# Self attention inside a pipelined perceiver layer: its scores on other PSUM banks and directly behind a step's logits, its softmax in two calls, its normalisations split from the products ahead of them

## The chip, the cores and the metric

One core of a Trainium2 chip runs the whole program. The metric is the time of one execution on the device, in microseconds. Three runs of the kernel before took 690.27 to 690.64 us, with a median of 690.4 us. Times inside an execution come from one profiled execution.

## The reference

The program computes one layer of a perceiver: a cross attention, a self attention and a quantised feed-forward net, each with a residual. The input x has 32 batches of 64 latents with 128 features; the context has 32 batches of 1601 tokens, of which a mask leaves out a part. All is float32.

```python
def cross(ctx, latents, mask):                   # 16 heads of 64
    xn, ln = layernorm(ctx, gx, bx), layernorm(latents, gl, bl)
    q, kv  = ln @ Wq, concatenate((xn, ln), axis=1) @ Wkv
    sim    = where(mask_full, -big, (q * scale) @ k.T)
    return layernorm((softmax(sim) @ v) @ Wout, go, bo)

def self_attention(x):                           # 16 heads of 8
    q, k, v = x @ Wq.T + bq, x @ Wk.T + bk, x @ Wv.T + bv
    scores  = q @ k.T / sqrt(8) + slopes * (pos_k - pos_q)
    return softmax(scores) @ v @ Wo.T + bo

x = x + cross(ctx, _layernorm(x), mask)
x = x + self_attention(_layernorm(x))
x = x + ffn(_layernorm(x))                       # fake-quantised, silu gate, 352 hidden
```

## The kernel before, in words

**Tiling.** Batches are sorted by how many context positions they need, and long ones are paired with short ones: 16 pairs of two batches, so that the 2 x 64 latents of a pair fill the 128 partitions. A batch is handled with a capped number of keys (its 64 latents among them): 448 for the first nine, 320 for eight, 192 for seven and 64 for the last eight. Pair t holds ranks t and 31 - t, so the early pairs have 448 and 64 keys, and the late ones 320 and 192. A switch chooses one of three variants of the whole attention by the lengths that the mask shows; this input takes the capped variant, called narrow in the code.

**PSUM.** All eight banks are given out by three rings: `bank_s` turns through two banks, `bank_t` and `bank_m` through three each. A call takes the next bank of its ring, and whoever writes into it first waits until the last reader of that bank's previous tile is done.

**Steps.** Pair t has eight steps, one for each two heads of the cross attention. The loop at L900 goes over all 128 steps and some more for the drain. In each it first calls `logits`, then the functions that a table `later` lists for that step, in the order in which they were listed. The framework turns this into one fixed instruction order for each engine, and sets the semaphores.

**The cross attention of a step.** `logits` multiplies the step's queries with the keys of each of the two batches (L568, PE, into a `bank_s` bank). VectorE adds the mask's addend and finds the row's least value while it evacuates the bank (L571, tile `s`, statistic `low`), ScalarE takes the exponential and sums it (L576, `den`), and VectorE inverts the sums and normalises (L582 `rden`, L585). Two steps later `turned` transposes the probabilities on PE (L604 for short batches, L614 for long ones, into `bank_t`), and ScalarE copies them out (L607, L615, tile `pT`). Another step or two later `attend` multiplies them with the normalised context (L632, into `bank_m`), and VectorE copies the product out (L637, `oT`).

**The next pair's preparation**, beside the steps of this pair: `latents` normalises its latents (`norm1`, L477, tile `ln`), `latents_T` transposes them (L243 from `ln`, into `bank_t`), `prepare` normalises its context tokens: VectorE takes the moments, L465 and GpSimd's power L469 give `rstd`, VectorE L498 gives `shift`, ScalarE applies both (L502), VectorE applies gain and bias (L224, L225), and GpSimd fills in the latents (L507) and turns the mask into addends (L510 to L520). `keys_T` transposes the tokens, `queries` multiplies the latents with the folded query weights (L544, four calls, into `bank_m`; ScalarE copies to `qT`, L548).

**The self attention of a finished pair** runs beside the steps of the next pair. Its pieces are put into the table by `chain`, a tuple of offsets from the step e in which the next pair begins: `project` in two calls (L663; behind the last come the moments of the product, gain and residual, L671 to L677, and a second normalisation to the tile `xl`, L680, with GpSimd's L469 in each), `self_T` (L689, transpose of `xl`), `self_qkv` (L700 to L728), `self_softmax` (L731), `self_pT` twice (transposes of the probabilities), `self_values` (L788, sums by L795) and `self_out` (L804, then a normalisation into `x3` and its largest absolute value for the quantisation, L806 to L809). `self_softmax` issues 8 small matmuls for scores into four banks (L738), one from `bank_s`, one from `bank_t` and two from `bank_m`; then, for each half of the 16 heads, two bias additions on VectorE (L750, tile `p`, each over four heads), a maximum (L754), a subtraction (L755) and an exponential on ScalarE (L759). For all pairs but the last two `chain` is

```python
elif t < NP - 2:
    chain = (4, 5, 7, 8, 10, 13, 14, 15, 16)
else:
    chain = (None, None, 4, 5, 6, 8, 8, 9, 10)
```

so that scores and softmax fall into step e + 10, the third step of the pair after the next. For the last two pairs the projection is spread over the pair's own steps in four parts. Behind the last step the feed-forward net follows, which needs the maximum over all pairs.

Of the kernel before, what the change touches and what calls it, by code (L numbers as in the profile page):

```python
# [8 lines left out]
FP = mybir.dt.float32  # L9
U8 = mybir.dt.uint8  # L10
I32 = mybir.dt.int32
AF = mybir.ActivationFunctionType
# [14 lines left out]
H = 16  # L27
# [10 lines left out]
def perceiver_layer(  # L38
# [21 lines left out]
    def bank_t():  # L60
        return ps_t.tile([P, 512], FP, tag="t", name="bank_t")

    def bank_m():
        return ps_m.tile([P, 512], FP, tag="m", name="bank_m")

    def bank_s():
        return ps_s.tile([P, 512], FP, tag="s", name="bank_s")
# [318 lines left out]
    def attention(actx, name, caps):  # L386
# [263 lines left out]
        def norm1(dst, src, twice=False):  # L650

            mean, rstd = moments(src, twice)
            nc.vector.tensor_scalar(dst, src, mean, rstd, ALU.subtract, ALU.mult)
# [4 lines left out]
        def project(t, part, parts=2):  # L658
            if part == 0:
                own[t] = bank_m()  # L660
            pm, oT = own[t], oTs[t]
            for h in range(H // parts * part, H // parts * (part + 1)):
                nc.tensor.matmul(  # L663
                    pm[:, :D], lhsT=oT[:, h].rearrange("p u i -> p (u i)"), rhs=b_sb[:, h, :],
                    start=(h == 0), stop=(h == H - 1),
                )
            if part < parts - 1:
                return
            oTs.pop(t)

            o = two.tile([P, D], FP, tag="o", name=f"o{t}")  # L671
            mean, rstd = moments(pm[:, :D])
            nc.vector.scalar_tensor_tensor(
                o, pm[:, :D], mean, go_r, ALU.subtract, ALU.mult
            )
            nc.vector.scalar_tensor_tensor(
                x1[:, t, :], o, rstd, x1[:, t, :], ALU.mult, ALU.add  # L677
            )
            xl = two.tile([P, D], FP, tag="xl", name=f"xl{t}")
            norm1(xl, x1[:, t, :])  # L680

            nc.gpsimd.tensor_tensor(x1[:, t, :], x1[:, t, :], sbo_r, ALU.add)
            own[t] = xl
# [44 lines left out]
                )  # L728
            own[t] = q, kx

        def self_softmax(t):  # L731
            q, kx = own[t]

            ps = [bank_s(), bank_t(), bank_m(), bank_m()]
            for u in range(2):
                for r in range(4):
                    rows = slice(32 * r, 32 * r + 32)
                    nc.tensor.matmul(  # L738
                        ps[r][u * SL : (u + 1) * SL, : 4 * SL],
                        lhsT=q[rows, u * SL : (u + 1) * SL],  # L740
                        rhs=kx[rows, :, u, :],
                        start=True, stop=True,
                    )
            p = two.tile([P, H, SL], FP, tag="p", name=f"p{t}", bufs=1)
            stat = small.tile([P, H], FP, tag="stat", name="stat")
            for g in range(2):
                hs = slice(g * 8, g * 8 + 8)
                for r in (2 * g, 2 * g + 1):
                    hr = slice(4 * r, 4 * r + 4)
                    nc.vector.tensor_tensor(  # L750
                        p[:, hr], ps[r][:, : 4 * SL].rearrange("p (h k) -> p h k", k=SL),
                        bias[:, hr], ALU.add,
                    )
                nc.vector.tensor_reduce(stat[:, hs], p[:, hs], AX.X, ALU.max)  # L754
                nc.vector.tensor_tensor(  # L755
                    p[:, hs], p[:, hs],
                    stat[:, hs].unsqueeze(2).to_broadcast([P, 8, SL]), ALU.subtract,
                )
                nc.scalar.activation(p[:, hs], p[:, hs], AF.Exp)  # L759
            own[t] = p  # L760

        def self_pT(t, g):

# [38 lines left out]
        def self_out(t):  # L802
            po = bank_m()
            nc.tensor.matmul(po[:, :D], lhsT=own.pop(t), rhs=swT[:, 3, :], start=True, stop=True)  # L804
            nc.vector.tensor_tensor(x1[:, t, :], po[:, :D], x1[:, t, :], ALU.add)
            norm1(x3[:, t, :], x1[:, t, :])  # L806
            nc.vector.tensor_reduce(
                tops[:, t : t + 1], x3[:, t, :], AX.X, ALU.max, apply_absolute_value=True
            )  # L809
# [20 lines left out]
        for t in range(NP):  # L830
            s0, e = CH * t, CH * (t + 1)
            if not narrow:
                chain = (4, 5, 9, 10, 12, 16, 17, 18, 19)
            elif t < NP - 2:
                chain = (4, 5, 7, 8, 10, 13, 14, 15, 16)
            else:
                chain = (None, None, 4, 5, 6, 8, 8, 9, 10)
            if chain[0] is None:
                for i in range(4):
                    at(s0 + 5 + 2 * i, project, t, i, 4)  # L840
            else:
                at(e + chain[0], project, t, 0)
                at(e + chain[1], project, t, 1)
            if t == NP - 1:
                for k in range(3):
                    at(e + chain[2], ffn_turn, k)
            for k, (f, *more) in zip(
                chain[2:],
                (
                    (self_T,), (self_qkv,), (self_softmax,), (self_pT, 0), (self_pT, 1),  # L850
                    (self_values,), (self_out,),
                ),
            ):
                at(e + k, f, t, *more)
            if t + 1 < NP:
                wait = 0 if narrow else 6
                at(s0 + wait, latents, t + 1)
                at(s0 + wait + 2, latents_T, t + 1)
                for i in range(4):
                    at(e - 6 + i if not narrow else e - 5 + i, queries, t + 1, 4 * i)  # L860

            if narrow:
                for u in range(2):
                    if t + 1 < NP:
                        at(s0 + 1 + 2 * u, prepare, t + 1, u)
                        at(s0 + 5 + u, keys_T, t + 1, u)
                    if t + 2 < NP:
                        at(s0 + 5, load, t + 2, u)
            else:
                for u in range(2):  # L870
                    if t + 1 < NP:
                        at(s0 + 2, lambda t, u: load_x(t, u, batch(t, u)), t + 1, u)
                    if (t, u) != (NP - 1, 1):
                        nxt = (t + u, 1 - u)
                        at(s0 + 8 * u + 3, load, *nxt)
                        at(s0 + 8 * u + 5, prepare, *nxt)
                        at(s0 + 8 * u + 6, keys_T, *nxt)
# [22 lines left out]
        for i in range(max(later) + 1):  # L900
            if i < len(steps):
                logits(*steps[i])
            for f, args in later.get(i, ()):
                f(*args)

    early.close()
# [158 lines left out]
```

## Time and profile before

| | |
|---|---|
| median of three runs | 690.4 us (690.27 to 690.64) |
| the profiled execution | 692.31 us |
| its span, first to last instruction | 690.3 us |
| mean granted TensorE clock | 0.961 |
| recorded instructions | 14206 |
| data moved by DMA | 11.98 MB |

The profiled execution lasted 2.0 us more than its span, which is start and end around the instructions; times inside it are counted from the span's first instruction. The page cuts the span into 40 slices of 17.3 us. A digit is the busy share of an engine in a slice in tenths, and PEclk is the clock that TensorE was granted, in tenths of full speed:

```profile
PE   4598999999998989898999999999999999954975
...
DVE  4487777787868797878778888888888778644673
ACT  2386667666675766675766767676766566512441
POOL 1338320211111112121111212020202000010002
PEclk9599999999999999999999999999999999975988
DMA  4520100000001010100000010000000000000002
```

The first two slices load and prepare, the slices from about the third to the 35th are the pairs, and the last ones are the drain of the last pair and the feed-forward net. PE, DVE, ACT and POOL are TensorE, VectorE, ScalarE and GpSimd. In the lines of a timeline the columns are: start in us, duration in us, engine, line, operation, output <- inputs, tile sizes, how many times in a row, and in brackets how long the engine was idle before it and what ended that. A row of the waits has an engine's tile and line that waited, what it waited for, and then the total in us, the number of times and the longest.

### The profile page before, as it was taken

The numbers are of one execution on the slowest core, as the hardware profiler recorded it, in microseconds if no ns is written. First come the engines' busy times: TensorE is split into PE (matmuls) and PEld (weight loads), VectorE is DVE, ScalarE is ACT, GpSimd is POOL, SyncE is SP. The second block draws the span as 40 slices with busy tenths as digits, with TensorE's granted clock in tenths as the row PEclk, the third lists the DMA queues.
The fourth block names the chain that finished last, engine by engine and source line by source line (L and its number), as shares of the span: only waits on it lengthen the run. The fifth ranks groups of instructions, "written<-read, shape, count | busy, mean of one in ns | idle before, by whom it ended". The sixth has DMA issues, their size and how long they took to land.

```text
span 690.3 us, 14206 instructions
## 1 busy us (share of the span) xinstructions
PE 620.7 (90%) x4798; PEld 496.9 (72%) x4798; DVE 518.7 (75%) x1992; ACT 409.8 (59%) x1096; POOL 130.0 (19%) x273
## 2 busy tenths in 40 slices
PE   4598999999998989898999999999999999954975
PEld 3576878777786868686878888888887886843335
DVE  4487777787868797878778888888888778644673
ACT  2386667666675766675766767676766566512441
POOL 1338320211111112121111212020202000010002
PEclk9599999999999999999999999999999999975988
DMA  4520100000001010100000010000000000000002
GB/s 103 118 56 0 25 1 24 2 24 1 24 2 23 2 30 1 24 1 20 5 11 14 11 15 8 18 7 19 5 24 1 1 1 1 1 1 3 1 0 62
DMA packets 20580, 11.98 MB, mean 17 GB/s; under 512 B 7748, under 2 KB 20036, under 8 KB 20500
## 3 DMA queue, kind: packets, MB, share of 16 engines
q1 hardware_dynamic: 19476, 10.02, 6.4%
q10 hardware_dynamic: 864, 0.82, 0.4%
q8 instruction: 40, 0.66, 0.4%
q14 instruction: 40, 0.33, 0.2%
q0 software_dynamic: 160, 0.16, 0.1%
HBM read 9.94 MB, written 1.05 MB: 16 GB/s over the span
## 4 chain that ended last, share of the span: by engine, by line
PE 49%; DVE 26%; ACT 8%; POOL 5%; issue 5%; DMA 2%; SPq 0%; POOLq 0%; DVEq 0%; ACTq 0%
PE bank_m L632 11%; PE bank_s L568 10%; PE bank_m L663 6%; PE bank_m L544 5%; ACT s L576 5%; DVE s L571 5%; POOL rstd L469 5%; DVE s L585 5%; PE bank_t L614 4%; PE bank_s L971 3%; PE bank_t L243 3%; DVE oT L637 2%; PE bank_m L998 2%; PE bank_t L604 2%; PE bank_m L788 1%
## 5 line engine op out<-in xcount | busy, mean ns | idle before, releaser
L576 ACT ACTIVATE s<-s,low 128x512 f32<-128x512 f32 (+3 forms) x256 | 143.8, 563 | 100.7 <-DVE low L571 87.5
L568 PE MATMUL bank_s<-xT,qT 128*128 128x512 f32 (+3 forms) x512 | 170.6, 449 | 20.6 <-DVE p L750 11.3
L632 PE MATMUL bank_m<-pT,xn 128*128 128x256 f32 x656 | 166.6, 381 | 1.6 <-ACT pT L615 1.4
L568 PEld LDWEIGHTS bank_s<-xT,qT 128*128 128x128 f32 x512 | 88.5, 194 | 77.8 <-DVE p L750 21.5
L469 POOL TENSOR_TENSOR rstd<-rstd,mhalf 128x1 f32<-128x1 f32 (+2 forms) x96 | 61.1, 638 | 411.7 <-DVE rstd L465 387.3
L632 PEld LDWEIGHTS bank_m<-pT,xn 128*128 128x128 f32 x656 | 118.2, 190 | 18.8 <-ACT pT L615 3.4
L571 DVE CUSTOM_DVE_ANT_0 s<-bank_s,ad 128x512 f32<-128x512 f32 (+3 forms) x256 | 121.0, 486 | 8.7 <-PE bank_s L568 7.9
L615 ACT COPY pT<-bank_t 128x512 f32<-128x512 f32 (+1 forms) x136 | 70.4, 523 | 51.5 <-PE bank_t L614 51.3
L585 DVE TENSOR_SCALAR s<-s,rden 128x512 f32<-128x512 f32 (+3 forms) x256 | 89.6, 391 | 2.0
L614 PE MATMUL bank_t<-ident,s 128*128 128x128 f32 x480 | 75.3, 273 | 0.0
L544 PE MATMUL bank_m<-lnT,a_sb 128*128 128x128 f32 x512 | 70.8, 284 | 0.4 <-ACT lnT L244 0.4
L614 PEld LDWEIGHTS bank_t<-ident,s 128*128 128x128 f32 x480 | 60.6, 141 | 13.6 <-issue 1.0
L544 PEld LDWEIGHTS bank_m<-lnT,a_sb 128*128 128x128 f32 x512 | 65.4, 201 | 0.7 <-ACT lnT L244 0.7
L663 PE MATMUL bank_m<-b_sb,oT 128*128 128x128 f32 x512 | 63.3, 276 | 0.5 <-DVE oT L637 0.5
L663 PEld LDWEIGHTS bank_m<-b_sb,oT 128*128 128x128 f32 x512 | 60.0, 192 | 1.7 <-DVE oT L637 1.3
L637 DVE COPY oT<-bank_m 128x256 f32<-128x256 f32 x128 | 53.2, 415 | 10.5 <-PE bank_m L632 10.2
L502 ACT ACTIVATE xn<-xn,shift,rstd 128x128 f32<-128x128 f32 x82 | 36.6, 490 | 25.5 <-DVE shift L498 25.4
L576 ACT ACTIVATION_READ_ACCUMULATOR s<-s,low 128x1 f32 x256 | 48.4, 189 | 0.0
L548 ACT COPY qT<-bank_m 128x512 f32<-128x512 f32 x64 | 37.4, 584 | 16.2 <-PE bank_m L544 15.8
L582 DVE RECIPROCAL rden<-den 128x2 f32<-128x2 f32 x128 | 20.4, 159 | 30.2 <-ACT s L576 29.4
L604 PE MATMUL bank_t<-ident,s 128*128 128x128 f32 x176 | 29.0, 273 | 0.0
L607 ACT COPY pT<-bank_t 128x256 f32<-128x256 f32 (+1 forms) x60 | 28.0, 466 | 0.0
(179 smaller groups left out, 853.5 us busy)
## 6 DMA issues: line engine op xcount, KB each, us to landing
xn<-in_ctx_dram SPq DMA_DIRECT2D x9, 192.0 KB, 2.4
x<-in_x_dram SPq DMA_DIRECT2D x32, 32.0 KB, 2.3
xn<-in_ctx_dram SPq DMA_DIRECT2D x32, 32.0 KB, 2.0
xn<-in_ctx_dram SPq DMA_DIRECT2D x8, 128.0 KB, 2.0
out_dram<-y SPq DMA_DIRECT2D x18, 32.0 KB, 1.9
wk_sb<-in_L_xattn_Wkv_dram ACTq DMA_DIRECT2D x1, 512.0 KB, 4.2
wq_sb<-in_L_xattn_Wq_dram SPq DMA_DIRECT2D x1, 512.0 KB, 5.1
wv_sb<-in_L_xattn_Wkv_dram SPq DMA_DIRECT2D x1, 512.0 KB, 5.3
```

The costliest lines, as they stand in the source:

```text
L469: nc.gpsimd.tensor_tensor(rstd, rstd, mhalf[:, :n], ALU.pow)
L544: nc.tensor.matmul(pm[:, j * P : (j + 1) * P], lhsT=a_sb[:, h4 + j, :], rhs=lnTs[t], start=True, stop=True,)
L568: nc.tensor.matmul(ps[:, : e - k], lhsT=w, rhs=xTs[t, u][:, k:e], start=True, stop=True)
L571: nc.vector.tensor_tensor_reduce(out=s[:, k:e], in0=ps[:, : e - k], in1=addends[u][t % NA][:, k:e], scale=-1.0, scalar=3e38 if j == 0 else ...
L576: nc.scalar.activation(s, s, AF.Exp, bias=low[:, len(pieces) - 1 :], scale=-1.0, accum_out=den[:, i : i + 1],)
L585: nc.vector.tensor_scalar_mul(s, s, rden[:, i : i + 1])
L604: nc.tensor.transpose(bt[:, n, o, :], s[:, n * P : (n + 1) * P], ident)
L614: nc.tensor.transpose(bt[:, j - n, :], s[:, j * P : (j + 1) * P], ident)
L615: nc.scalar.copy(pT[:, n:e, odd, :], bt[:, : e - n, :])
L632: nc.tensor.matmul(po[:, : 2 * P], lhsT=xn[:k, n, :], rhs=pT[:k, n].rearrange("p o c -> p (o c)"), start=(n == 0), stop=(n == len(tiles) - 1),
L637: nc.vector.tensor_copy(oTs[t][:, 2 * c : 2 * c + 4, u, :], po[:, : 2 * P].rearrange("p (h i) -> p h i", i=SL),)
L663: nc.tensor.matmul(pm[:, :D], lhsT=oT[:, h].rearrange("p u i -> p (u i)"), rhs=b_sb[:, h, :], start=(h == 0), stop=(h == H - 1),)
```

## The change

Four things are done. `project` no longer issues the normalisations behind its product; a new function `project_norm` does, listed directly behind the second call and in the same step. Likewise `ffn_norm` takes the normalisation and maximum out of `self_out`, in the same step. `self_softmax` is split: `self_scores` issues the score matmuls and all four bias additions, and takes two `bank_t` and two `bank_m` banks and none of `bank_s`; `self_softmax(t, g)` issues maximum, subtraction and exponential of one half, with a statistics tile of its own, in step e + 11 where the pieces stood in e + 10 (for the last two pairs in e + 6, as the scores). And the loop over steps puts `self_scores` ahead of all other functions of its step, so it comes directly behind the logits. The offsets of all the other pieces are as before. The other variants' offsets change alike; they don't run on this input.

```diff
--- before.py
+++ after.py
@@ -664,9 +664,11 @@
                     pm[:, :D], lhsT=oT[:, h].rearrange("p u i -> p (u i)"), rhs=b_sb[:, h, :],
                     start=(h == 0), stop=(h == H - 1),
                 )
-            if part < parts - 1:
-                return
-            oTs.pop(t)
+            if part == parts - 1:
+                oTs.pop(t)
+
+        def project_norm(t):
+            pm = own[t]
 
             o = two.tile([P, D], FP, tag="o", name=f"o{t}")
             mean, rstd = moments(pm[:, :D])
@@ -728,10 +730,10 @@
                 )
             own[t] = q, kx
 
-        def self_softmax(t):
+        def self_scores(t):
             q, kx = own[t]
 
-            ps = [bank_s(), bank_t(), bank_m(), bank_m()]
+            ps = [bank_t(), bank_t(), bank_m(), bank_m()]
             for u in range(2):
                 for r in range(4):
                     rows = slice(32 * r, 32 * r + 32)
@@ -742,22 +744,24 @@
                         start=True, stop=True,
                     )
             p = two.tile([P, H, SL], FP, tag="p", name=f"p{t}", bufs=1)
-            stat = small.tile([P, H], FP, tag="stat", name="stat")
-            for g in range(2):
-                hs = slice(g * 8, g * 8 + 8)
-                for r in (2 * g, 2 * g + 1):
-                    hr = slice(4 * r, 4 * r + 4)
-                    nc.vector.tensor_tensor(
-                        p[:, hr], ps[r][:, : 4 * SL].rearrange("p (h k) -> p h k", k=SL),
-                        bias[:, hr], ALU.add,
-                    )
-                nc.vector.tensor_reduce(stat[:, hs], p[:, hs], AX.X, ALU.max)
+            for r in range(4):
+                hr = slice(4 * r, 4 * r + 4)
                 nc.vector.tensor_tensor(
-                    p[:, hs], p[:, hs],
-                    stat[:, hs].unsqueeze(2).to_broadcast([P, 8, SL]), ALU.subtract,
-                )
-                nc.scalar.activation(p[:, hs], p[:, hs], AF.Exp)
+                    p[:, hr], ps[r][:, : 4 * SL].rearrange("p (h k) -> p h k", k=SL),
+                    bias[:, hr], ALU.add,
+                )
             own[t] = p
+
+        def self_softmax(t, g):
+
+            p = own[t]
+            stat = small.tile([P, H // 2], FP, tag="stat", name="stat")
+            hs = slice(g * 8, g * 8 + 8)
+            nc.vector.tensor_reduce(stat, p[:, hs], AX.X, ALU.max)
+            nc.vector.tensor_tensor(
+                p[:, hs], p[:, hs], stat.unsqueeze(2).to_broadcast([P, 8, SL]), ALU.subtract
+            )
+            nc.scalar.activation(p[:, hs], p[:, hs], AF.Exp)
 
         def self_pT(t, g):
 
@@ -803,6 +807,8 @@
             po = bank_m()
             nc.tensor.matmul(po[:, :D], lhsT=own.pop(t), rhs=swT[:, 3, :], start=True, stop=True)
             nc.vector.tensor_tensor(x1[:, t, :], po[:, :D], x1[:, t, :], ALU.add)
+
+        def ffn_norm(t):
             norm1(x3[:, t, :], x1[:, t, :])
             nc.vector.tensor_reduce(
                 tops[:, t : t + 1], x3[:, t, :], AX.X, ALU.max, apply_absolute_value=True
@@ -830,11 +836,11 @@
         for t in range(NP):
             s0, e = CH * t, CH * (t + 1)
             if not narrow:
-                chain = (4, 5, 9, 10, 12, 16, 17, 18, 19)
+                chain = (4, 5, 5, 9, 10, 12, 12, 12, 16, 17, 18, 19, 19)
             elif t < NP - 2:
-                chain = (4, 5, 7, 8, 10, 13, 14, 15, 16)
+                chain = (4, 5, 5, 7, 8, 10, 11, 11, 13, 14, 15, 16, 16)
             else:
-                chain = (None, None, 4, 5, 6, 8, 8, 9, 10)
+                chain = (None, None, 3, 4, 5, 6, 6, 6, 8, 8, 9, 10, 10)
             if chain[0] is None:
                 for i in range(4):
                     at(s0 + 5 + 2 * i, project, t, i, 4)
@@ -843,12 +849,13 @@
                 at(e + chain[1], project, t, 1)
             if t == NP - 1:
                 for k in range(3):
-                    at(e + chain[2], ffn_turn, k)
+                    at(e + chain[3], ffn_turn, k)
             for k, (f, *more) in zip(
                 chain[2:],
                 (
-                    (self_T,), (self_qkv,), (self_softmax,), (self_pT, 0), (self_pT, 1),
-                    (self_values,), (self_out,),
+                    (project_norm,), (self_T,), (self_qkv,), (self_scores,), (self_softmax, 0),
+                    (self_softmax, 1), (self_pT, 0), (self_pT, 1), (self_values,), (self_out,),
+                    (ffn_norm,),
                 ),
             ):
                 at(e + k, f, t, *more)
@@ -900,7 +907,8 @@
         for i in range(max(later) + 1):
             if i < len(steps):
                 logits(*steps[i])
-            for f, args in later.get(i, ()):
+
+            for f, args in sorted(later.get(i, ()), key=lambda x: x[0] is not self_scores):
                 f(*args)
 
     early.close()
```

Line numbers behind L666 differ by up to 8 in the changed kernel: the scores' matmuls are L740 there, the bias additions L749, maximum L760, subtraction L761, exponential L764.

## The prediction

> **What bounds the kernel now.** I read the page's busy rows and chain first, then who waits for whom on PE, then the timelines of two pairs: an early one (448 and 64 keys, 135.5 to 171.6) and a late one (320 and 192 keys, 430 to 500).
>
> ```profile
> PE 620.7 (90%) x4798; PEld 496.9 (72%) x4798; DVE 518.7 (75%) x1992; ACT 409.8 (59%) x1096; POOL 130.0 (19%) x273
> ...
> PE 49%; DVE 26%; ACT 8%; POOL 5%; issue 5%; DMA 2%; SPq 0%; POOLq 0%; DVEq 0%; ACTq 0%
> ```
>
> PE is busiest, yet half of the chain that ended last lies elsewhere. PE's two largest repeated waits are these (total, times, longest):
>
> ```profile
> PE bank_s L568 <- DVE p L750: 11.3, 12, 1.3
> PE bank_s L568 <- DVE low L571: 9.0, 10, 1.8
> ```
>
> The first is what the change is aimed at: logits need a ps_s bank that the self attention's scores hold until VectorE has added the bias. The second shows something else: logits that wait for VectorE's previous evacuation. Both stand in each early pair:
>
> ```profile
> 136.82 1.35 PE L568 MATMUL bank_s<-xT,qT 128*128 128x512 f32 x4 [0.86 <-DVE low L571]
> ...
> 142.79 0.49 PE L568 MATMUL bank_s<-xT,qT 128*128 128x128 f32 x2 [1.05 <-DVE p L750]
> ```
>
> Now VectorE in that pair:
>
> ```profile
> 142.35 0.39 DVE L750 TENSOR_TENSOR p<-bank_s,bias 128x256 f32<-128x256 f32 x1
> ...
> 152.35 0.16 DVE L498 SCALAR_TENSOR_TENSOR shift<-mv,rstd 128x4 f32<-128x4 f32 x1 [1.20 <-POOL rstd L469]
> ...
> 154.94 0.17 DVE L582 RECIPROCAL rden<-den 128x2 f32<-128x2 f32 x1 [1.27 <-ACT s L576]
> ...
> 156.55 0.69 DVE L224 TENSOR_TENSOR xn<-xn,gx_r 128x512 f32<-128x512 f32 x1 [0.73 <-ACT xn L502]
> ...
> 159.25 0.68 DVE L571 CUSTOM_DVE_ANT_0 s<-bank_s,ad 128x512 f32<-128x512 f32 x1
> ...
> 161.29 0.35 DVE L653 TENSOR_SCALAR xl<-x,mv,rstd 128x128 f32<-128x128 f32 x1 [0.67 <-POOL rstd L469]
> 161.56 0.16 DVE L582 RECIPROCAL rden<-den 128x2 f32<-128x2 f32 x1
> ```
>
> It works 28.6 of 36.1 us, and the other 7.5 are round trips to ScalarE and GpSimd; not once does it wait for PE. So in an early pair the loop VectorE, ScalarE, GpSimd sets the 36.1 us, and PE, with 34.2 busy, fits in. A late pair (34.6 us, PE busy 33.7) is the reverse: PE's only gap is the 0.86 below, and VectorE does wait for PE.
>
> ```profile
> 467.25 0.70 PE L568 MATMUL bank_s<-xT,qT 128*128 128x256 f32 x2 [0.86 <-DVE p L750]
> ```
>
> ```profile
> 458.05 0.42 DVE L637 COPY oT<-bank_m 128x256 f32<-128x256 f32 x1 [0.57 <-PE bank_m L632]
> ...
> 466.80 0.39 DVE L750 TENSOR_TENSOR p<-bank_s,bias 128x256 f32<-128x256 f32 x1
> ```
>
> **The change, part by part.** No instruction is added or removed: per pair 32 score matmul halves, four bias adds (0.33 each from start to start), two maxima (0.59), two subtractions (0.60), two exponentials (0.53). DMAs and SP's queue stay as they are; GpSimd only swaps two neighbouring copies once. The split-off normalisations run in the same step as before, so the code moves nothing by them; what moves is the order on each engine, read from the built program. In the cost of work: 0.
>
> Scores on PE now stand right behind their step's logits, ahead of the attention products and transposes: 0.61 us earlier in the queue by 1.8 to 2.2 us. Their four groups take two ps_t and two ps_m banks. The wait does not vanish: the three ps_t banks rotate, and the third allocation after the first score group is the transpose of the next latents (L243 from ln). It stands on PE directly ahead of the logits that used to wait. So the new wait is this transpose's, for the first bias add; the following L632 waits for the third add, and L544 for the fourth. Behind the transpose is queued all of PE, and so VectorE.
>
> *Weighed against a rule.* The Trainium skill (Perfetto Trace Analysis, Identifying Performance Opportunities) says that the same gap, repeating on the engine that should be saturated, can mean that too little PSUM is left for the next tile. By that rule, taking the scores out of ps_s gains all of the row's 11.3 us: 679.1. But 2 + 3 + 3 banks of one 512-column tile were in use before and are after; the hold moves to another ring. I therefore take what the ring's next user has to wait, worked out below.
>
> Early pair, from 135.47 (PE has done L604; all equal until there). Logits start at 136.82 as before. Scores end at 138.5, L632 (1.73) at 140.25, four transposes (0.44) at 140.7. VectorE: L477 and rden now precede the evacuation, which starts at 138.80 (138.51 before); 0.61 + 0.62 (L585) + 0.20 bring it to 140.24, so the first add is done at 140.65. PE does not wait, and L632 starts at 141.9 instead of 143.12: 1.2 ahead. Then it gives this back twice.
> - ScalarE now has the exponentials of logits step 3 ahead of the pT copy (L615) that PE needs next. Those logits' evacuation comes behind adds, rden, L585, oT and maximum: 140.24 + 4 x 0.33 + 0.12 + 0.08 + 0.62 + 0.33 + 0.59 = 143.30, plus 0.68. Exponentials of 0.72 and 0.39 follow, then the copy, to 145.8. PE is there at 145.1: 0.7 idle.
> - The qT copy (L548) now stands behind L502, which waits for GpSimd's rstd, and all four L502 stand before the exponentials of step 5. These start at 154.75 (153.72 before), the next pT copy ends at 156.4 (155.37), and the xn transposes, ready at 155.9, wait until 156.5 (156.31 before).
>
> PE's lead is gone. On VectorE, L465 for the shift comes at 151.16 (151.01): same work, 0.15 more in short waits. L224 then finds its L502 earlier (154.9), so the projection's moments start at 157.0 with both affine steps done. But the built order puts the evacuation of step 6 behind xl instead of into it. With the distances of the trace from moments to xl's end (0.32 + 0.22 + 0.82 + 0.38 + 0.33 + 0.22 + 0.81 + 0.26 = 3.36) it starts at 160.36, not 159.25. rden follows an evacuation by 0.79 + 1.23, at 162.4 instead of 161.56, and L585, without L637 between to cover its latency, at 162.57 instead of 161.95. From there to the next pair's first evacuation nothing changes. So: 0.6 us longer per pair. The order has this form in four early pairs: 4 x 0.6 = 2.4. One further pair (the seventh) moves the evacuation likewise: 0.4.
>
> Late pair. PE: logits end at 463.08, scores 463.7, L632 (1.30) 465.0, three transposes 465.3; then ln's transpose waits. VectorE's path from 458.05, where it waits for PE, is nearly gapless; L585 starts at 465.6 (its rden ends 465.49), takes 0.6, the first add is done at 466.6. PE restarts at 466.66, with 0.11 of restart as at 467.25 in the trace; L243 0.11 and logits 1.08 bring L632 to 467.96 instead of 467.79. The gap of 0.86 has become one of 1.35 in another place: 0.17 longer, six times, 1.0.
>
> The remaining pairs (the first, sixth, eighth and fifteenth) I put at 0; bounds: a gain of their whole wait (0.8 to 1.3 each), or a loss of the early pair's 0.6.
>
> Tail, last pair, nothing beside it: VectorE's order becomes four adds, two maxima, two subtractions. The first exponential starts at 622.6 instead of 622.0, the second as before, and PE does the second half's transposes behind the first half's: 0.3. Bounds 0 and 0.6.
>
> Sum: 2.4 + 0.4 + 1.0 + 0.3 = 4.1. The profiled execution took 692.3 (span 690.3, 2.0 around it), so 696.4 for its like; on the median of 690.4, 694.5.
>
> **Rivals.**
> - *Slower, mainly so* (0.66): the above. Worst, if every one of 14 pairs pays 0.7 and the tail 0.3: 10.1, to 700.5.
> - *Faster* (0.22), one mechanism: the first add comes before PE reaches ln's transpose, in late pairs too, and PE keeps its lead. For: in the early pair it does, by 0.05, and late pairs are bound by PE. Against: VectorE has no gap ahead of that add in a late pair. It decides at 1.35 us earlier for the add; half of it wins 5.0 (685.4), all of it 11.3 (679.1).
> - *The same* (0.12): the wait moves ring and nothing else; late 0, and ScalarE's reordering is absorbed in early pairs. For: PE had 1.9 idle in each. 690.4.
>
> The range 685.5 to 700.5 reaches into the faster case and to the worst of the slower. A difference under 0.2% (1.4 us) is about what a measurement of this kernel cannot tell from none.
>
> **What would show it.** Right: no L568 waits for a bias add; instead L243 of ln waits for it in late pairs, by 1.2 to 1.4; early pairs at 36.5 to 36.9 from add to add, late ones at 34.7 to 34.9; L571 of step 6 behind xl; PE's waits for low L571 grow. Wrong: late pairs at 33.8, or early pairs under 36.0, that is, VectorE's loop is shorter in the new order than my distances say.

## The result, and the profile after

The changed kernel takes as long as the kernel before: medians of 691.13 and 690.77 us over 12 runs each, ratio 0.9994 with a 95% interval of 0.998 to 1.0008. The forecast was 694.5, slower. The page of the profiled execution (689.49 us, span 687.8), its busy row and its chain:

```profile
PE 625.0 (91%) x4798; PEld 500.4 (73%) x4798; DVE 521.8 (76%) x1992; ACT 410.0 (60%) x1096; POOL 128.9 (19%) x273
...
PE 62%; DVE 20%; issue 5%; ACT 4%; POOL 4%; DMA 1%; SPq 0%; POOLq 0%; DVEq 0%; ACTq 0%
```

The chain now runs through PE for 62% of the span instead of 49%. PE's waits (total, times, longest):

```profile
PE bank_t L243 <- DVE p L749: 5.1, 5, 1.2
PE bank_s L568 <- DVE low L571: 4.7, 6, 1.4
...
PE bank_s L568 <- DVE rstd L465: 3.7, 4, 1.3
...
PE bank_t L614 <- DVE p L749: 1.5, 2, 1.0
```

No logits wait for a bias add any more (11.3 before). Transposes do instead, for 5.1 and 1.5. The rows that end in low L571 and in rstd L465 are one kind of wait, of logits for the previous evacuation, with L465 its neighbour on VectorE; together they are 8.4 here and 9.3 before. An early pair on PE: the transpose of ln goes through unhindered, and one short wait for ScalarE's copy follows.

```profile
139.36 0.27 PE L243 MATMUL bank_t<-ident,ln 128*128 128x128 f32 x1
...
143.96 1.99 PE L632 MATMUL bank_m<-pT,xn 128*128 128x256 f32 x8 [0.19 <-ACT pT L615]
```

The same pair on VectorE:

```profile
138.62 0.74 DVE L749 TENSOR_TENSOR p<-bank_t,bias 128x256 f32<-128x256 f32 x2
...
149.01 0.15 DVE L465 TENSOR_SCALAR rstd<-mv 128x4 f32<-128x4 f32 x1
150.36 0.16 DVE L498 SCALAR_TENSOR_TENSOR shift<-mv,rstd 128x4 f32<-128x4 f32 x1 [1.20 <-POOL rstd L469]
...
154.84 0.29 DVE L645 BATCH_NORM_STATS2 st<-bank_m 128x6 f32<-128x128 f32 x1
...
158.21 0.68 DVE L571 CUSTOM_DVE_ANT_0 s<-bank_s,ad 128x512 f32<-128x512 f32 x1
```

A late pair on PE, where ln's transpose is what waits:

```profile
462.49 0.33 PE L243 MATMUL bank_t<-ident,ln 128*128 128x128 f32 x1 [0.98 <-DVE p L749]
```

And the last pair, three waits of PE:

```profile
569.76 0.55 PE L614 MATMUL bank_t<-ident,s 128*128 128x128 f32 x3 [0.97 <-DVE p L749]
...
589.40 0.98 PE L614 MATMUL bank_t<-ident,s 128*128 128x128 f32 x7 [0.52 <-DVE p L749]
...
620.50 1.97 PE L243 MATMUL bank_t<-ident,p 128*128 128x128 f32 x8 [4.10 <-ACT p L764]
```

**Pair by pair.** To see where time went I take the starts of the evacuations (L571) from the trace and measure each pair from its first evacuation to the next pair's. Pair t has 448 and 64 keys up to t = 7, 448 and 192 at t = 8, then 320 and 192, and 320 and 320 at t = 15.

| pair t | 3 | 4 | 5 | 6 | 7 | 8 | 9 | 10 | 11 | 12 | 13 | 14 | 15, to the FFN |
|---|---|---|---|---|---|---|---|---|---|---|---|---|---|
| before | 36.10 | 36.10 | 36.10 | 36.85 | 35.88 | 39.19 | 36.87 | 34.53 | 34.65 | 34.60 | 35.54 | 35.75 | 70.95 |
| after | 36.12 | 36.41 | 36.12 | 35.90 | 35.99 | 37.92 | 35.85 | 34.61 | 34.81 | 34.71 | 35.20 | 36.27 | 72.24 |

The last column ends where PE transposes the FFN's first maximum. Pairs 0 to 2 agree within 0.11. From the first evacuation to that point, called the common stretch below, it is 598.1 before and 597.0 after: pairs 6, 8 and 9 gain 3.2, pair 14 and the last one lose 1.8, the rest is small. What lies outside the stretch (start and FFN) has the same instructions in both kernels and is not compared: its length follows the granted clock (last section).

### The profile page after: what moved, and what is told of

It is laid out like the page before. It is cut to its first block, busy times and chain, and to the rows that moved or that the text cites. A ratio compares the mean times of both kernels' runs of the same rounds, so it can differ in the third digit from the quotient of the medians.

```text
span 687.8 us, 14193 instructions
## 1 busy us (share of the span) xinstructions
PE 625.0 (91%) x4798; PEld 500.4 (73%) x4798; DVE 521.8 (76%) x1992; ACT 410.0 (60%) x1096; POOL 128.9 (19%) x273
## 3 DMA queue, kind: packets, MB, share of 16 engines
HBM read 9.94 MB, written 1.05 MB: 16 GB/s over the span
## 4 chain that ended last, share of the span: by engine, by line
PE 62%; DVE 20%; issue 5%; ACT 4%; POOL 4%; DMA 1%; SPq 0%; POOLq 0%; DVEq 0%; ACTq 0%
PE bank_m L632 14%; PE bank_s L568 12%; PE bank_m L663 8%; PE bank_m L544 7%; PE bank_t L614 5%; PE bank_t L243 4%; DVE s L585 4%; DVE s L571 3%; ACT s L576 3%; POOL rstd L469 3%; PE bank_s L979 3%; PE bank_m L792 2%; PE bank_t L604 2%; PE bank_m L1006 2%; DVE p L749 2%
## 5 line engine op out<-in xcount | busy, mean ns | idle before, releaser
L568 PE MATMUL bank_s<-xT,qT 128*128 128x512 f32 (+3 forms) x512 | 165.4, 444 | 8.5 <-DVE low L571 4.7
L571 DVE CUSTOM_DVE_ANT_0 s<-bank_s,ad 128x512 f32<-128x512 f32 (+3 forms) x256 | 119.2, 488 | 8.6 <-PE bank_s L568 7.9
L614 PE MATMUL bank_t<-ident,s 128*128 128x128 f32 x480 | 74.3, 273 | 1.5 <-DVE p L749 1.5
L614 PEld LDWEIGHTS bank_t<-ident,s 128*128 128x128 f32 x480 | 60.2, 141 | 17.4 <-DVE p L749 2.3
L604 PE MATMUL bank_t<-ident,s 128*128 128x128 f32 x176 | 29.1, 273 | 0.0
```

What stands on the lines that cost most here:

```text
L568: nc.tensor.matmul(ps[:, : e - k], lhsT=w, rhs=xTs[t, u][:, k:e], start=True, stop=True)
L571: nc.vector.tensor_tensor_reduce(out=s[:, k:e], in0=ps[:, : e - k], in1=addends[u][t % NA][:, k:e], scale=-1.0, scalar=3e38 if j == 0 else ...
L604: nc.tensor.transpose(bt[:, n, o, :], s[:, n * P : (n + 1) * P], ident)
L614: nc.tensor.transpose(bt[:, j - n, :], s[:, j * P : (j + 1) * P], ident)
```

## The experiments

The change has three parts that can be set one by one: the first score group on a bank_t bank instead of a bank_s bank (banks), maximum to exponential a step after the adds (later), and scores right behind the logits (placed).

| kernel | banks | later | placed | t=4 | t=8 | t=11 | common stretch | median | ratio, 95% interval |
|---|---|---|---|---|---|---|---|---|---|
| before | | | | 36.10 | 39.19 | 34.65 | 598.1 | 690.8 | 1 |
| changed | x | x | x | 36.41 | 37.92 | 34.81 | 597.0 | 691.1 | 0.9994 (0.998 to 1.0008) |
| banks alone | x | | | 36.12 | 38.89 | 34.53 | 597.1 | 690.4 | 0.9981 (0.997 to 0.9992) |
| bank_s again | | x | x | 36.88 | 39.00 | 34.53 | 600.9 | 694.8 | 1.0043 (1.0033 to 1.0054) |
| unplaced | x | x | | 35.68 | 38.35 | 33.89 | 589.0 | 682.1 | 0.9853 (0.9818 to 0.9888) |
| same step | x | | x | 36.24 | 38.77 | 34.91 | 600.9 | 695.4 | 1.0053 (1.004 to 1.0066) |
| later alone | | x | | 36.03 | 38.84 | 34.68 | 595.4 | 689.3 | 0.9961 (0.9947 to 0.9976) |
| same step, unplaced | x | | | 36.10 | 39.09 | 34.65 | 598.1 | 691.9 | 1.0012 (1.0002 to 1.0021) |

The last row differs from "banks alone" in that its four adds stand together, as they do in all rows below "banks alone" and in the changed kernel. The ratios are to runs of the kernel before made beside each experiment; the medians of these were 691.2 to 691.5.

One reservation on the stretch: it includes most of the drain's time at half clock (last section). From the last 30 of PE's products with `unit`, the sums of the last `self_values`, to the FFN's first maximum the traces of before and changed both take 6.78 us, at clock 0.50; the unplaced kernel's takes 6.24 at 0.77 and that of "later alone" 6.07 at 0.78. These two stretches are shorter by 0.5 and 0.7 for the clock alone. In that of "later alone" the first pair, with 3.4 us at half clock, is 0.6 longer and makes up for it.

My theory A at the start was that the banks win what the waits of PE show and that only the placing gives it back.

**Banks alone.**

```diff
-            ps = [bank_s(), bank_t(), bank_m(), bank_m()]
+            ps = [bank_t(), bank_t(), bank_m(), bank_m()]     # in the kernel before
```

> The kernel before with one edit: the first score group takes a bank_t bank, no bank_s bank. Theory A (what the placing ahead of the step's other work gave away): without that placing the third bank_t allocation after the first score group is not the transpose of ln but the next step's short transposes (L604), which PE reaches late enough; so the logits' wait for the bias add goes and nothing takes its place. Late pairs 33.8 us instead of 34.6, the pair with 448 and 192 keys 37.9 instead of 39.2, early pairs 36.1 as before (they are not bound by PE), drain from the last pair's first evacuation 128.0 as before: sum about -7, 683.5, ratio 0.990. Rival B (a hold only moves from ring to ring): some bank_t or bank_m allocation waits for the same add, late pairs 34.6, ratio 1.000. Rival C (the order on VectorE, adds together and exponentials a step later, made what was gained in the changed kernel): no gain here either, ratio 1.000.

Ratio 0.9981: theory A's -7 us did not come. The wait for the add is gone, as A said, but two others took its place. PE's waits in this kernel, and the two in a late pair:

```profile
PE bank_s L568 <- DVE low L571: 11.5, 17, 1.8
...
PE bank_t L243 <- ACT pT L615: 5.2, 11, 0.8
```

```profile
430.31 0.33 PE L243 MATMUL bank_t<-ident,ln 128*128 128x128 f32 x1 [0.27 <-ACT pT L615]
...
435.06 0.91 PE L568 MATMUL bank_s<-xT,qT 128*128 128x384 f32 x2 [0.39 <-DVE low L571]
```

So 0.27 goes to ln's transpose, which waits for ScalarE to empty the bank_t bank ahead of the scores', and 0.39 to logits that wait for the previous evacuation (L571): that one stands behind adds, maxima and subtractions in VectorE's queue. Of the 0.86 only 0.2 is left, and the pair is 0.12 shorter.

**bank_s again, in the changed kernel.**

```diff
-            ps = [bank_t(), bank_t(), bank_m(), bank_m()]
+            ps = [bank_s(), bank_t(), bank_m(), bank_m()]
```

> The changed kernel with the first score group on a bank_s bank again. Theory A: the second of the next step's logits waits for the first add again, but the add is earlier than in the kernel before, and ln's transpose waits no longer; late pairs 34.0 to 34.6 (the logits that wait stand 0.65 us behind ln's transpose, so of the wait of 0.98 in the changed kernel some 0.35 stay), early pairs 36.1 to 36.4, drain 129.4 as in the changed kernel: ratio 0.996. Rival B: the same wait in the other ring, late pairs 34.7, ratio 1.000. Rival C: as the changed kernel, 1.000.

1.0043, which none of the three theories gave. Late pairs came out as A said (34.5), but the early ones are at 36.6 to 36.9, where A had 36.1 to 36.4. A score group placed right behind the logits on a bank_s bank waits for the evacuation of those same logits:

```profile
PE bank_s L740 <- DVE low L571: 8.1, 13, 1.3
```

**Unplaced: the changed kernel without the placing.**

```diff
-            for f, args in sorted(later.get(i, ()), key=lambda x: x[0] is not self_scores):
+            for f, args in later.get(i, ()):
```

> The changed kernel without the placing: scores stand in their step behind the attention products and transposes, as before; banks, the four adds together and the exponentials a step later are kept. Theory A: as in the banks-only kernel ln's transpose no longer waits for the add: late pairs 33.8, the pair with 448 and 192 keys 37.9, early pairs 36.1 to 36.4; the drain keeps part of what it lost (128.5 to 129.4). Ratio 0.991. Rival B: late pairs 34.7, ratio 1.000. Rival D (what was gained came from the placing, because the adds come early by it): worse than the changed kernel, ratio 1.003.

0.9853, faster than any theory said, so rivals B and D fall. Early pairs are at 35.68, late ones at 33.89. A late pair on PE: ln's transpose now waits for ScalarE's copy and only 0.34.

```profile
458.00 0.33 PE L243 MATMUL bank_t<-ident,ln 128*128 128x128 f32 x1 [0.34 <-ACT pT L615]
```

In the unplaced order the step's own transposes take their bank ahead of the scores, so ln gets the bank that they used, and the bank held for the first add falls to the long batch's transposes (L614) two products further on. (The expectation under Banks alone names L604; by the order of the calls that is the allocation behind it.) An early pair on VectorE:

```profile
148.75 0.15 DVE L465 TENSOR_SCALAR rstd<-mv 128x4 f32<-128x4 f32 x1
148.81 0.17 DVE L582 RECIPROCAL rden<-den 128x2 f32<-128x2 f32 x1
149.01 0.70 DVE L585 TENSOR_SCALAR s<-s,rden 128x512 f32<-128x512 f32 x2
150.09 0.16 DVE L498 SCALAR_TENSOR_TENSOR shift<-mv,rstd 128x4 f32<-128x4 f32 x1 [0.38 <-POOL rstd L469]
```

Here a reciprocal and two normalisations fill GpSimd's round trip between L465 and L498: 0.38 of waiting, where both the kernel before and the changed one wait 1.20. The order that the placing leads to has that work ahead of L465 instead.

**Same step: the softmax back in the scores' step, in the changed kernel.**

```diff
-                chain = (4, 5, 5, 7, 8, 10, 11, 11, 13, 14, 15, 16, 16)
+                chain = (4, 5, 5, 7, 8, 10, 10, 10, 13, 14, 15, 16, 16)
```

> The changed kernel with maximum, subtraction and exponentials in the step of the scores, as before, for all pairs but the last two. Theory A: the step behind matters little: late pairs 34.7 (the first add's time is the same, and PE waits for that alone), early pairs within 0.3 of 36.2, drain 129.4: ratio 1.000. Rival C: the later exponentials are what helps the pairs between; the pair with 448 and 192 keys goes back to 39.2 and its neighbours by 1 each: ratio 1.004.

1.0053: A is wrong here and rival C close. Pair 8 goes back to 38.8 and pair 9 to 36.9 (35.9 in the changed kernel), with PE's waits for the previous evacuation at 12.0 instead of 8.4. So in the changed kernel the step behind is worth some 4 us.

After these four I dropped A for a theory of two locks. PE's logits need a free bank, and they need VectorE's last evacuation. The banks open the first, the step behind opens the second, and with one shut nothing goes through. The next two runs open one each without the placing.

**Later alone.**

```diff
-            ps = [bank_t(), bank_t(), bank_m(), bank_m()]     # in the unplaced kernel
+            ps = [bank_s(), bank_t(), bank_m(), bank_m()]
```

> The split and the halves a step behind alone: scores stand in their step as before, and their first group is on a bank_s bank as before. Theory A (early pairs are bound by VectorE, whose next evacuation no longer stands behind maxima and subtractions; late pairs need the bank as well): early pairs 35.7 to 35.8 instead of 36.1, late pairs 34.5 instead of 34.6, as the second of the next logits still waits 0.8 for the first add; drain 128.8; sum -3.0, ratio 0.996. Rival E (banks and step behind give what the unplaced kernel gains only together, since both act on the same evacuation): early pairs 36.1, ratio 1.000.

The ratio, 0.9961, is A's, but not by its reason: early pairs stay at 36.03, where rival E has them. The bank still costs what it did:

```profile
PE bank_s L568 <- DVE p L749: 10.7, 12, 1.1
...
PE bank_s L568 <- DVE low L571: 7.4, 8, 1.4
```

The early pair on VectorE also sets right what the unplaced kernel seemed to say of it:

```profile
187.27 0.16 DVE L498 SCALAR_TENSOR_TENSOR shift<-mv,rstd 128x4 f32<-128x4 f32 x1 [0.27 <-POOL rstd L469]
187.89 0.69 DVE L571 CUSTOM_DVE_ANT_0 s<-bank_s,ad 128x512 f32<-128x512 f32 x1 [0.46 <-PE bank_s L568]
```

The wait for GpSimd is short here too, and the pair is still at 36.03: the next evacuation now waits 0.46 for PE, whose logits were held for the add. So VectorE's order is one lock of the early pair, and PE's bank the other.

**Same step, unplaced.**

```diff
-                chain = (4, 5, 5, 7, 8, 10, 11, 11, 13, 14, 15, 16, 16)     # in the unplaced kernel
+                chain = (4, 5, 5, 7, 8, 10, 10, 10, 13, 14, 15, 16, 16)
```

> The unplaced kernel (new banks, four adds together) with maximum, subtraction and exponential back in the step of the scores. Theory A: the next evacuation is behind the softmax again: early pairs 36.1, late pairs 34.4 to 34.5 as with the banks alone, drain 128.8: ratio 0.998. Rival F (that the four adds stand together frees the banks sooner, and this is what counts): as the unplaced kernel, early 35.7, late 33.9, ratio 0.986.

1.0012: early pairs as A said, late ones 0.2 worse, and rival F (adds together) falls. In the early pairs L498 waits 0.27 and the evacuation behind it 0.46 for PE, as in "later alone". This is the other lock:

```profile
PE bank_s L568 <- DVE low L571: 14.0, 24, 1.4
```

So banks alone save 0.2%, later alone 0.4%, both 1.5%: the two locks are shown. PE's waits in this part of a late pair say the same: 0.27 and 0.39 with the banks alone, 0.85 with later alone, 0.26 and 0.56 here, and only 0.33 with both. In early pairs too neither alone gives more than 0.07, and both give 0.42.

**What the placing costs, stage by stage.** Against the unplaced kernel the changed one loses 8.0 us in the common stretch: 0.3 to 0.7 in each of pairs 3 to 7, 0.5 to 0.9 in pairs 10 to 14, 2.2 in the last (0.5 of it the clock's, as said), while pairs 8 and 9 gain 0.5 together. Three runs take these apart. First the late pairs: the changed kernel, with ln's transpose on a bank_s bank.

```diff
-            transposed(lnT.unsqueeze(1), [lns[t]], nc.scalar.copy)
+            bt = bank_s()
+            nc.tensor.transpose(bt[:, :P], lns[t], ident)
+            nc.scalar.copy(lnT, bt[:, :P])
```

> The changed kernel (scores placed right behind the logits, two bank_t and two bank_m banks); only the transpose of ln takes a bank_s bank instead of a bank_t bank. Theory A (in late pairs the placing costs what the ring costs: this transpose is the third bank_t allocation behind the first score group): the wait of 0.98 goes, of which the attention product behind the logits, which waits for the third add, takes back 0.3 at most; late pairs 33.8 to 34.1 instead of 34.75; early pairs stay at 36.1 to 36.4, since there VectorE's order sets the time; drain 129.4. Sum -4, ratio 0.994. Rival I (the placing costs by what it delays on VectorE and PE, whatever the banks): late pairs 34.7, ratio 1.000.

0.996 (0.9946 to 0.9975), late pairs 34.1 to 34.3, early ones as before this edit, as A said. (The stretch of the profiled execution, 597.1, doesn't show the gain: its first pair is 1.7 longer, a part of it at half clock.) The wait of 0.98 is gone and 0.48 of it won, less than the 0.65 to 0.95 of A. The rest went into rows that show no idle time (this edit moves lines by 2):

```profile
463.36 1.54 PE L570 MATMUL bank_s<-xT,qT 128*128 128x384 f32 x4
465.05 1.13 PE L634 MATMUL bank_m<-pT,xn 128*128 128x256 f32 x4
```

From start to start these four logits take 1.69, and 1.08 elsewhere. A narrower window splits these 0.61:

```profile
464.20 0.70 PE L570 MATMUL bank_s<-xT,qT 128*128 128x256 f32 x2
```

The second batch's two logits, due at 464.00 (0.32 behind each of the first two), start at 464.20, when ScalarE's copy of ln has left their bank (it ends at 464.15), and the first of them takes 0.10 longer: 0.30. The other 0.31 are L634's wait for the third add, which the list of waits names in pairs 13 and 14. So the ring accounts for about half of the late pairs' 0.9.

The early pairs: the fastest kernel (below) with the placing for the scores of pairs 0 to 4 only, which fall into pairs 2 to 6.

```diff
-            for f, args in later.get(i, ()):
+            for f, args in sorted(
+                later.get(i, ()), key=lambda x: x[0] is not self_scores or x[1][0] > 4
+            ):
```

> The unplaced kernel with the last two pairs as before (the fastest so far), with the placing only for the scores of the second to fifth pair. Theory A (in the early pairs the placing costs through VectorE's order, since GpSimd's round trip for the token statistics is then waited for in full): the four early pairs 36.1 to 36.4 instead of 35.66, all later pairs as in the unplaced kernel (35.3, 38.4, 35.9, 33.9): 1.8 to 2.4 more, ratio 0.988 to 0.989. Rival L (early pairs lose only by what the placing does in the pairs around them): 35.7, ratio 0.9855.

Pairs 3 to 6 take 36.13, 36.43, 36.12 and 35.91, against 35.66, 35.67, 35.66 and 35.59: 2.0 more, as A said, and the wait of 1.20 at L498 is back. Rival L falls. Pair 2 stays at 33.73 (33.78). The ratio, 0.9905 (0.9887 to 0.9923), is 1 to 2 us above A's; in the trace pair 13 has 0.65 of it and the FFN, with the same instructions, 2.0.

The last pairs: the changed kernel, but unplaced and with the old softmax order in the last two pairs.

```diff
+                if t >= NP - 2 and r % 2:          # in self_scores, behind the add of group r
+                    self_softmax(t, r // 2)
...
-            for f, args in sorted(later.get(i, ()), key=lambda x: x[0] is not self_scores):
+            for f, args in sorted(
+                later.get(i, ()), key=lambda x: x[0] is not self_scores or x[1][0] >= NP - 2
+            ):
```

> The changed kernel, but for the last two pairs: their scores are not placed ahead, and their softmax is issued as in the kernel before. Theory A (in the drain the placing holds two bank_t banks that the transposes of the last pair wait for, and four adds ahead of the first maximum make the last exponentials late): of the two waits of transposes for a bias add in the drain (0.97 and 0.52) the second goes, which belongs to the last pair but one; the wait for the last exponential falls from 4.1 to 3.4; so 1.0 to 1.4 less than the changed kernel, ratio 0.998; pairs before the drain unchanged (36.1 to 36.4, 34.7). Rival K (the drain's loss is a difference of single executions, as the clock there is lowered for a while at varying places): ratio as the changed kernel, 0.9994 or above.

0.998 (0.9969 to 0.999), as A said: the last pair takes 71.26 to the FFN instead of 72.24, PE's wait for the exponential is 3.44 again, the transposes' wait of 0.52 is gone and that of 0.97 still there. Rival K's 0.9994 lies outside the interval, and the clock over the last pair is the same in both traces (0.85 and 0.86).

**Towards a faster kernel.** The unplaced kernel with the old softmax order in the last two pairs (the first two lines of the last diff):

> The unplaced kernel; only in the last two pairs the softmax is issued as in the kernel before: two adds, maximum, subtraction, exponential, then the second half. Theory A: the drain from the last pair's first evacuation takes 128.0 again instead of 128.8, all else as in the unplaced kernel: 0.8 less, ratio 0.984. Rival G (the drain's loss comes from the new banks and not from the order): 128.8, ratio 0.985.

681.34 us, 0.9855 (0.9839 to 0.9872), the fastest of all; the unplaced kernel's 0.9853 rests on four runs that lie wider, so the two can't be told apart by their ratios. In the trace PE's wait for the last exponential is 3.44 instead of 4.04, but the eight transposes behind it then take 2.38 instead of 1.97, so they end only 0.19 earlier; and the last pair takes 70.41 instead of 70.07, as the unplaced trace has the better clock there. So A's 0.8 was not seen, and G is not excluded.

Two edits aimed at ln's wait for ScalarE's copy (5.4 in the unplaced kernel). One moves that transpose, and the queries behind it, by a step in the unplaced kernel:

```diff
-                at(s0 + wait + 2, latents_T, t + 1)
+                at(s0 + wait + 2 + narrow, latents_T, t + 1)
...
-                    at(e - 6 + i if not narrow else e - 5 + i, queries, t + 1, 4 * i)
+                    at(e - 6 + i if not narrow else e - 4 + i, queries, t + 1, 4 * i)
```

> The unplaced kernel with the transpose of ln, and the queries that need it, one step later. Theory A (what is left of PE's idle time in late pairs is the bank that this transpose shares with ScalarE's pT copy): that wait (0.33 in late pairs, 0.8 in early ones) goes; late pairs 33.6 instead of 33.9, early pairs unchanged at 35.7 as they are bound by VectorE: -2, ratio 0.982. Rival H (the queries then collide with the projection's bank_m hold and qT comes late): late pairs 34.5 or more, ratio 0.990.

1.0012 (1.0002 to 1.0022), late pairs 34.5: H's time for them, but neither its ratio (0.990) nor its mechanism, as no query waits for a bank_m bank; PE's logits wait for L571 16.0 us in all instead of 8.6, 3.3 of it in the first pair. Why that evacuation comes late here is open. The other puts the transpose on a bank_s bank in the fastest kernel (the diff with `bt = bank_s()` above):

> The unplaced kernel with the last two pairs' softmax as before, and the transpose of ln on a bank_s bank, to take away its wait for ScalarE's copy (0.34 in late pairs, 0.79 in early ones). Theory A: late pairs 33.6 instead of 33.9, early pairs unchanged at 35.7 since VectorE sets them: -1.5 to -2, ratio 0.983. Rival J (the next logits, which now share a ring with the transpose, wait for ScalarE's copy of ln instead): late pairs 33.9 or more, ratio 0.986 or above.

682.5 us, 0.9868 (0.9852 to 0.9885), late pairs 33.88 as without it: rival J's time, but not its way. The transpose's wait left the list, and the logits behind it follow at once. The 0.34 so won is lost 5 us further on, where the attention products of the next step start 1.32 behind their logits (462.10 and 463.42) instead of 1.08, and the first of them takes 0.10 longer: they wait for ScalarE's copy of pT, which ends at 463.37. The higher median is not the late pairs' either; in the trace the first pair is 1.0 longer than without the edit.

## Why the prediction was wrong

Two terms of the sum failed: VectorE's path in the early pairs, which was to lose 0.15 us on the way to L465 and won 0.37, and the pairs put at 0 or near it, of which three gained about 1 us each. In the traces the evacuation of step 6 moves behind xl in pairs 2 to 5 and 7, counted from 0; these are the forecast's four early pairs and its seventh.

| pairs | forecast | measured |
|---|---|---|
| 2 to 5 | 2.4 longer | 0.2 longer |
| 7 | 0.4 longer | 0.1 longer |
| 1, 6 and 8 | 0 | 2.2 shorter |
| 9 to 14 | 1.0 longer | 0.5 shorter |
| 15, the tail | 0.3 longer | 1.3 longer |
| sum | 4.1 longer | 1.1 shorter |

Times below are from a pair's first evacuation.

- *PE's wait moves to ln's transpose.* Right. In late pairs it is 0.98 there, forecast 1.35; pairs 10 to 12 are 0.08, 0.16 and 0.11 longer, forecast 0.17.
- *Early pair, first half.* Right in its order: the first add starts at 10.09 (forecast 10.08), the third step's evacuation at 13.00 (13.14). PE then waits 0.19 for the copy, where 0.7 was forecast.
- *"On VectorE, L465 for the shift comes at 151.16 (151.01): same work, 0.15 more in short waits."* This step failed. It is 20.48 into the pair (149.01), where before it was 20.85 and the forecast means 21.00. The moments follow at 26.31 instead of the forecast 26.84, and the evacuation of step 6, which does stand behind xl, at 29.68 instead of 30.20 (29.09 before). The half microsecond that VectorE won earlier pays for what the order costs, so pairs 3 to 5 are 0.02 to 0.31 longer and not 0.6. PE's waits for the previous evacuation, which were to grow, fell from 9.3 to 8.4.
- *"The remaining pairs … I put at 0".* This failed too, and so did the 0.17 for pair 9: pairs 6, 8 and 9 gain 0.95, 1.27 and 1.02. In pair 8 the row of before was 1.27 for the add and in pair 9 it was 0.96; with the changed kernel both are gone, and ln's transpose finds its bank free. But that alone is not the gain. With the softmax in the scores' step ("same step") the transpose doesn't wait either, and PE then waits 0.69 and 0.74 for L571 in these pairs, which are at 38.77 and 36.86: a gain of 0.42 and of nothing. The step behind, which had no term of its own in the forecast, is what wins the rest. Pair 6 is another case: it is at 36.03 with "later alone" already, where its logits still wait 1.05 for the add. What it gains by is open.
- *Tail, 0.3.* Measured 1.3. PE's wait for the first of the last exponentials is 0.66 longer (4.10 against 3.44), for the reason given, but the transposes behind it end only 0.25 later for that, which is the 0.3 of the forecast. The other 1.04 are there when the last scores start: the two transposes that wait 0.97 and 0.52 for bank_t banks in this pair were missed, though it is the same ring as in the late pairs.
- *The rivals.* The result is that of *the same*, but not its way: it is gains and losses of 1 us each that cancel, which is chance. *Faster* has the right pairs in 8 and 9, where the wait is won, but not the second condition.
- *The rule on gaps that repeat.* PE's waits for the add fell from 11.3 to 6.6 with the changed kernel, and the time not at all; unplaced they are gone, and 9.1 of the common stretch with them (8.6 without the clock's 0.5). The rule's 679.1 is near what the fastest kernel reaches, 681.3, but the bank alone, which is all that the rule names, gave 0.2%.
- Two slips bear on nothing: the traces have 16 score matmul records in a pair and not 32, and half of 11.3 is 5.6 and not 5.0.

What I did not ask was what each part of the change is worth without the others. The placing, which I took as given, costs what the other two parts win.

## What to carry to other kernels

A wait in the profile shows only the lock that opens last: when an engine needs both a free buffer and another engine's last result, test the removal of both together before giving up either. When a tile is moved to another ring of banks, follow that ring's allocations in program order, and see who comes next and how soon; moving work forward in the program also moves its place in the ring. Judge a change with several parts by switching each off, since a flat result can be a gain and a loss.

## What the runs showed of the hardware

The granted clock of TensorE falls to half for a while in each profiled execution here, and when it does so is not the same. The columns are the stretch, its length, busy time (and instructions) of PE, its loads, DVE, ACT and POOL, then the granted clock, the DMA share and GB/s. At the start, before:

```profile
17.00:35.00 18.00, 10.56 (x41) 8.98 (x42) 8.14 (x35) 5.48 (x14) 6.19 (x16) 0.53 0.54 115
```

and after, and then after in the drain:

```profile
17.00:35.00 18.00, 10.55 (x50) 8.95 (x51) 9.12 (x41) 6.08 (x16) 6.28 (x17) 0.91 0.55 116
```

```profile
610.00:636.00 26.00, 11.94 (x113) 9.11 (x114) 11.83 (x34) 6.68 (x13) 1.66 (x4) 0.50 0.01 3
```

The first evacuation came at 35.15 before and 33.64 after, with the same instructions ahead of it, so over half of the 2.8 us between the two profiled executions says nothing of the change. In the drain the clock is at half for 26 us while PE is busy under half of the time; between the two the windows show 1.00. The Trainium skill (TensorE: Matmul & The Clock Gate, What's actually happening) has the clock fall to half after an idle window of about 3.4 us. The drain's half clock does begin in an idle time, PE's wait of 3.8 us for xl, but 1.4 us (before) and 2.2 us (after) into it, so sooner than that. For a change of a few tenths of a per cent this was reason enough to compare pairs and not spans.

Also unexpected: an idle time that leaves the list of waits need not leave the time. With ln's transpose on a bank_s bank pairs 10 to 12 listed no wait in either kernel, and pair 11 stayed at 33.88 in one of them and won 0.48 of 0.98 in the other; the time was in rows that count as busy, and showed in the distance from one start to the next.
